# Ends of a sparse GATv2 layer: three per half block where there were five

## The chip, the cores and the metric

The kernel runs on one core of a Trainium2 chip. The metric is the device time of one execution in microseconds, as the median of ten runs: 3402.1 us before the change, with 3391.11 us the lowest and 3414.27 us the highest.

## What is computed

Two graph layers over 3327 nodes with 128 features, on one weighted adjacency matrix (`adj`, about 2% of its entries are not zero, the diagonal among them). The first is a GATv2 layer with four heads, the second a normalized graph convolution. Cut to what matters:

```python
h = maximum(layernorm(x), 0)
for each head:                      # w1, w2, a, Wlin of the head
    E = leaky_relu((h @ w1)[:, None, :] + (h @ w2)[None, :, :], 0.01)
    s = exp(tanh((E @ a) / 8) * 8) * adj
    s = s / sum(s, -1)
    out = leaky_relu(s @ h @ Wlin.T, 0.01)
x = x + concat(outs) @ w
# second layer
h = maximum(layernorm(x), 0)
x = x + relu(A_norm @ (h @ W.T + b))     # A_norm of adj + identity
```

## The kernel before

The rows are cut into 26 blocks of 128, and each block into two half blocks of 64 rows. For each row the kernel makes a list of its neighbours (`prep`, spread over the block before), and then works only on edges.

Each half block has five **parts**. Parts 0 to 3 hold 16 listed edges of each row each; part 4 holds the extra edges of rows with more. For parts 0 to 3, eight indirect DMAs on GpSimd (POOL, L595) gather 128 rows of a table in HBM, some 364 KB each, into one of four buffers `g`; part 4 has one buffer `ge`, two gathers and one plain DMA. A gathered row holds the features, the products with w2, a linear part of the score and the adjacency weights.

A half block is worked in nine **groups** `m`: parts 0 to 3 have two each (m = 0 to 7), part 4 has m = 8. For a group, `stage_z` turns the gathered rows (16 TensorE transposes, L622) into two PSUM tiles `z`, and VectorE takes the maximum with the row's own part into `r` (L638; ScalarE and VectorE share this for m = 8, L635 and L633). `stage_r` multiplies `r` by the vector `a` (L657). It does so for two groups at once, and a half group late: the scores of m = 0 and 1 are issued in the middle of group 2. One score matmul has two columns of weights, takes 512 columns of `r` and writes two PSUM rows for one head; four heads lie in four bands of 32 rows of one bank `s`, which is kept for the whole kernel. Row 0 is of the first group, row 1 of the second:

```python
for at, r in ((0, k.held), (1, rs)) if at else ((0, rs),):
    for h in range(H):
        nc.tensor.matmul(k.s[32 * h:32 * h + 2, :n], sel[:, h, 31 - at:33 - at], r[h // 2][:, h % 2, :n],
                         start=(at == 0), stop=(at == 1 or m == 8))
```

After each part comes its **end**, `finish`, a generator. It copies the bank to SBUF (`ssb`, ScalarE, L666), transposes it (L675, four matmuls, three for part 4), adds the linear parts (`sc`, VectorE, L678 and L681), takes tanh and exp (ScalarE, L686 and L688), multiplies with the adjacency weights (`wq` and `wt`, L670 and L697; `am` and `wo`, L713 and L715, for part 4), and multiplies with the gathered features into the PSUM tile `ag` (TensorE, L706, or L724 for part 4). Then `allow` gives the gather buffer back, and the next gather into it can be issued.

The order of instructions is written by hand. `slot()` is called six times for each group; it takes one step of every open generator (`tails`, `ends`), then of `prep`, then starts fetches for which a buffer is free. A `yield` in an end is one slot of distance: the products L706 stand twelve slots behind the start of their end, five of them behind `wt`. A fetch is made in the fixed order of blocks, halves and parts.

Other work in the same queues: `prep` transposes a block of `adj` (L365) and copies it out (`at`, ScalarE, L367, then a DMA from ScalarE's queue, L370); `known_step` uses `at` on TensorE (L379); `weights` writes a block's weights into the table (a DMA on SP's queue, L605); `close` ends a half block (L735 to L797). After the last block the second layer's strips come in through the same four buffers `g` (L898, from SP's and ScalarE's queues) and are multiplied (L988).

Of the kernel before, what the change touches and what calls it, by code (L numbers as in the profile page):

```python
# [9 lines left out]
F32 = mybir.dt.float32  # L10
AF = mybir.ActivationFunctionType
OP = mybir.AluOpType
# [3 lines left out]
P = 128  # L16
SLOPE = 0.01
CAP = 8.0
EPS = 1e-5
BANK = 512  # L20
# [42 lines left out]
OVT = 3  # L63
FOUND = 2
FEAT = 64
BODY = 648
# [3 lines left out]
WIDE = 712  # L70
WORK = 133
# [160 lines left out]
def _sparse_layers(tc, nc, x, adj, w1, w2, a, wlin, w, gw, gb, gb_sb, gwT, x_sb, dinv, flag, ident, out):  # L232
# [13 lines left out]
    NP, D = x.shape  # L246
    H = w1.shape[0]
# [4 lines left out]
    NG = 9  # L252
    WT = 8
    NW = NT // WT
    LATE = 1

    with ExitStack() as l0:
        res = l0.enter_context(tc.tile_pool(name="res", bufs=1))
# [9 lines left out]
        w1_sb = res.tile([P, H, D], F32, name="w1_sb")  # L268
        wlinT = res.tile([P, H, D], F32, name="wlinT")
        w_sb = res.tile([P, H, D], F32, name="w_sb")  # L270
        sel = res.tile([P, H, 33], F32, name="sel")
        p_all = res.tile([P, NB, 2 * H], F32, name="p_all")
        code = res.tile([P, NP], mybir.dt.uint16, name="code")
        epos = res.tile([P, 2 * FOUND], F32, name="epos")
# [3 lines left out]
        qmask = res.tile([P, 8], F32, name="qmask")  # L278
# [365 lines left out]

        def stage_r(k, hb, m, rs):
            n = 4 * P if m < 8 else FOUND * P + HALF
            at = m % 2
# [4 lines left out]
            if at == 0 and m < 8:  # L652
                k.held = rs
                return
            for at, r in ((0, k.held), (1, rs)) if at else ((0, rs),):
                for h in range(H):
                    nc.tensor.matmul(k.s[32 * h:32 * h + 2, :n], sel[:, h, 31 - at:33 - at], r[h // 2][:, h % 2, :n],  # L657
                                     start=(at == 0), stop=(at == 1 or m == 8))


        def finish(k, hb, w):
            g, s = k.g.pop((hb, w)), k.s
            f0 = k.f0[hb]
            nt, nk, nm = (WT, 4, 2) if w < NW else (OVT, OVT, 1)
            ssb = ph.tile([P, BANK], F32, name="ssb", bufs=1)
            nc.scalar.copy(ssb[:, :nk * P], s[:, :nk * P])  # L666
            if w < NW:
                wq = pb.tile([P, WT, 8], F32, name="wq")
                diag = bass.AP(g.tensor, g.offset + BODY * hb, [list(g.ap[0]), [WIDE + 8, 8], [1, 8]])
                nc.vector.tensor_tensor(wq, diag, qmask[:, None, :].to_broadcast([P, WT, 8]), OP.mult)  # L670
            yield
            yield
            pt = ps_tr.tile([P, 4, P], F32, name="tr")
            for q in range(nk):
                nc.tensor.transpose(pt[:, q, :], ssb[:, q * P:(q + 1) * P], ident)  # L675
            yield
            sc = pb.tile([P, WT, H], F32, name="sc")
            nc.vector.tensor_tensor(sc[:, :nt].rearrange("p (m k) h -> p m k h", m=nm),  # L678
                                    pt.rearrange("p k (h m) -> p m k h", m=32)[:, :nm, :nk],
                                    g[:, :, f0 + D:f0 + D + H].rearrange("p (m k) h -> p m k h", m=nm), OP.add)  # L680
            nc.vector.tensor_add(sc[:, :nt], sc[:, :nt], k.pex[:, 8 * hb:8 * hb + 8] if w < NW else  # L681
                                 k.ex[:, OVT * hb:OVT * hb + OVT, 42:42 + H])
            yield
            yield
            th = pb.tile([P, WT, H], F32, name="th")
            nc.scalar.activation(th[:, :nt], sc[:, :nt], AF.Tanh, scale=1.0 / CAP)  # L686
            pe = pb.tile([P, WT, H], F32, name="pe")
            nc.scalar.activation(pe[:, :nt], th[:, :nt], AF.Exp, scale=CAP)  # L688
            yield
            yield  # L690

            if w == 0:
                k.ag = ps_a.tile([P, 2, 256], F32, name="ag")
            ag = k.ag
            if w < NW:
                wt = pv.tile([P, WT, H, 8], F32, name="wt", bufs=2)
                nc.vector.tensor_tensor(wt, pe[:, :, :, None].to_broadcast([P, WT, H, 8]),  # L697
                                        wq[:, :, None, :].to_broadcast([P, WT, H, 8]), OP.mult)
                yield
                yield  # L700
                yield
                yield
                yield
                for t in range(WT):
                    u, cg = t // 4, t % 4
                    nc.tensor.matmul(ag[32 * cg:32 * cg + 32, u, :WORK], wt[:, t].rearrange("p h q -> p (h q)"),  # L706
                                     g[:, t, f0:f0 + WORK], start=(w == 0 and t < 4), stop=False, skip_group_check=True)
                allow("g")
                return
            am = pb.tile([P, OVT, HALF], F32, name="am", bufs=1)  # L710
            wo = pv.tile([P, OVT, 8, H, 8], F32, name="wo")
            for t in range(OVT):
                nc.vector.scalar_tensor_tensor(am[:, t, :], code[:, :HALF], k.ex[:, OVT * hb + t, 41:42], g[:, t, BODY * hb:BODY * hb + HALF],  # L713
                                               op0=OP.is_equal, op1=OP.mult)
                nc.vector.tensor_tensor(wo[:, t], pe[:, t, None, :, None].to_broadcast([P, 8, H, 8]),  # L715
                                        am[:, t].rearrange("p (g q) -> p g q", q=8)[:, :, None, :].to_broadcast([P, 8, H, 8]), OP.mult)
# [10 lines left out]
            tails.append(close(k, hb))  # L727


        def close(k, hb):  # L730
# [71 lines left out]
        blks = []  # L802
        for b in range(NB):
            k = Blk()
            k.f0 = FEAT, 0
            k.g, k.b, k.ready, k.turned, k.closed = {}, b, False, False, False
            blks.append(k)
        NCODE = 20
        NLIST = 42
        NPREP = 72  # L810
# [7 lines left out]
        ends, tails = [], []  # L818
# [183 lines left out]
        with tc.tile_pool(name="pre", bufs=1) as pre, ExitStack() as images:  # L1002
# [11 lines left out]
            room = [images.enter_context(tc.tile_pool(name=f"image{i}", bufs=1)).tile(  # L1014
                        [P, min(4, NB - 4 * i), BODY], F32, name=f"img{i}") for i in range(-(-NB // 4))]
# [176 lines left out]
        with tc.manual_schedule():  # L1192
            fetch()
            while queue:
                issue()
            rs = {}
            n = len(groups)
            def scores(i):
                if 0 <= i < n:
                    b, hb, m = groups[i]  # L1200
                    stage_r(blks[b], hb, m, rs.pop(i))
                    if m % 2 or m == NG - 1:
                        ends.append(finish(blks[b], hb, m // 2))
# [160 lines left out]
```

## Time and profile before

| | |
|---|---|
| median of ten runs | 3402.1 us (3391.11 to 3414.27) |
| the profiled execution | 3406.0 us, span 3404.3 us |
| mean granted TensorE clock | 0.88 |
| PE, PEld, DVE, ACT, POOL busy | 78%, 55%, 62%, 20%, 50% |
| DMA, mean | 243 GB/s, 826.94 MB moved |
| gathers on POOL (L595, `g`) | 1664 x 954 ns |
| maximum into `r` (L638) | 832 x 1218 ns |
| copy of the bank (L666) | 260 x 564 ns |
| transposes of the ends (L675) | 988, 172.2 us busy |
| products (L706) | 3328, 235.8 us busy |

PE is TensorE's matmuls, PEld its weight loads, DVE VectorE, ACT ScalarE. A group's line gives the line of the kernel, engine, operation, what is written from what, the number of instructions, then the busy time and the mean of one in ns, then the idle time of the engine just before them with what ended it. In a timeline a row gives start and length in us and, in brackets, the idle time before. An fp32 score matmul counts twice in the number of instructions.

### The profile page before, as it was taken

What the parts mean: (1) busy time and instruction counts of PE and PEld (TensorE: products, weight loads), DVE (VectorE), ACT (ScalarE), POOL (GpSimd) and SP (SyncE); (2) the same over time, 40 slices, a digit from 0 to 9 for tenths busy, and PEclk for the clock granted to TensorE, in tenths of its full rate; (3) what the DMA queues carried; (4) which work ended last, traced back from release to release, by engine and by line L of the source; (5) the groups of instructions that cost most, each with busy time, mean ns of one, the idle gap of its engine ahead of it and who ended that gap; (6) DMA issues with size and microseconds to landing.
All of it is one profiled execution on the core that took longest, in us unless ns stands there. A gap on an engine that the chain in (4) does not pass through costs nothing.

```text
span 3404.3 us, 52385 instructions
## 1 busy us (share of the span) xinstructions
PE 2641.9 (78%) x19410; PEld 1857.6 (55%) x19410; DVE 2099.0 (62%) x6426; ACT 683.0 (20%) x1703; POOL 1710.3 (50%) x1822
## 2 busy tenths in 40 slices
PE   6687777787777877787787777777787777777887
PEld 4465555555555555565555555555555555555553
DVE  6676666657656666666665665665665665665442
ACT  3122122212212212221121121221221221221110
POOL 3555555555555555545545545545545445445520
PEclk8788889988989889889888888988988888898999
DMA  9977778678777767867867867777777777777886
GB/s 325 319 253 260 227 249 268 216 238 275 234 227 262 253 214 251 263 202 251 268 201 244 264 209 237 255 226 227 251 231 224 250 234 222 231 223 222 268 257 185
DMA packets 417844, 826.94 MB, mean 243 GB/s; under 512 B 38435, under 2 KB 288815, under 8 KB 414255
## 3 DMA queue, kind: packets, MB, share of 16 engines
q0 software_dynamic: 141440, 619.41, 55.6%
q1 hardware_dynamic: 165343, 147.87, 14.1%
q10 hardware_dynamic: 110800, 56.25, 5.6%
q8 instruction: 156, 2.56, 0.3%
q14 instruction: 105, 0.86, 0.1%
HBM read 754.47 MB, written 113.22 MB: 255 GB/s over the span
## 4 chain that ended last, share of the span: by engine, by line
PE 51%; DVE 17%; issue 11%; another core or an unknown queue 11%; DMA 5%; POOL 3%; ACT 1%; ACTq 0%; SPq 0%; DVEq 0%; POOLq 0%
PE z L622 18%; PE s L657 10%; DVE r L638 9%; PE ag L706 5%; POOL g L595 3%; PE z L627 3%; PE tr L675 2%; DVE cand L422 2%; PE tr L379 2%; PE ag L724 2%; DMA g<-table,idx 2%; DMA g<-AT_d 1%; PE z L988 1%; PE tr L523 1%
## 5 line engine op out<-in xcount | busy, mean ns | idle before, releaser
L595 POOL DMA_INDIRECT g<-table,idx x1664 | 1588.1, 954 | 1361.4 <-PE ag L706 789.4
L638 DVE TENSOR_TENSOR r<-z,x1n 128x1024 f32<-128x1024 f32 x832 | 1013.0, 1218 | 871.0 <-remote 390.9
L622 PE MATMUL z<-ident,g 128*128 128x128 f32 x6656 | 1062.6, 305 | 182.4 <-issue 121.6
L622 PEld LDWEIGHTS z<-ident,g 128*128 128x128 f32 x6656 | 870.0, 159 | 366.1 <-issue 246.8
L657 PE MATMUL s<-r,sel 128*2 128x512 f32 (+1 forms) x3744 | 545.7, 609 | 134.9 <-DVE r L638 96.0
L666 ACT COPY ssb<-s 128x512 f32<-128x512 f32 x260 | 146.6, 564 | 843.7 <-PE s L657 303.2
L706 PE MATMUL ag<-g,wt 128*32 128x133 f32 x3328 | 235.8, 309 | 96.1 <-issue 95.3
L657 PEld LDWEIGHTS s<-r,sel 128*2 128x2 f32 x3744 | 82.6, 84 | 400.2 <-issue 254.3
L706 PEld LDWEIGHTS ag<-g,wt 128*32 128x32 f32 x3328 | 137.5, 119 | 219.9 <-issue 210.5
L675 PE MATMUL tr<-ident,ssb 128*128 128x128 f32 x988 | 172.2, 300 | 94.4 <-issue 76.3
L422 DVE MAX8 cand<-codes 128x8 f32<-128x52 uint16 x1664 | 217.3, 204 | 0.0
L675 PEld LDWEIGHTS tr<-ident,ssb 128*128 128x128 f32 x988 | 129.2, 155 | 120.4 <-issue 101.1
L595 POOL DMA_INDIRECT ge<-table,idxo x104 | 99.1, 952 | 182.6 <-PE ag L724 91.7
L379 PE MATMUL tr<-at,x_sb 128*128 128x128 f32 x488 | 99.2, 361 | 115.1 <-ACT at L367 109.6
L367 ACT COPY at<-tr 128x512 f32<-128x512 f32 (+1 forms) x175 | 97.2, 555 | 421.3 <-remote 219.5
L379 PEld LDWEIGHTS tr<-at,x_sb 128*128 128x128 f32 x488 | 83.4, 255 | 142.0 <-ACT at L367 130.9
L686 ACT ACTIVATE th<-sc 128x32 f32<-128x32 f32 x260 | 58.4, 225 | 499.0 <-DVE sc L681 234.7
L633 DVE TENSOR_TENSOR r<-z,x1n 128x128 f32<-128x128 f32 x104 | 30.1, 290 | 193.0 <-PE z L627 135.0
L365 PE MATMUL tr<-ident,adjb 128*128 128x128 f32 x676 | 124.3, 311 | 31.1 <-DMA adjb<-in_adj_dram 16.4
L627 PE MATMUL z<-oi,x1b 128*128 128x256 f32 x416 | 134.9, 408 | 4.0 <-issue 4.0
L453 DVE MAX8 lists<-cand 128x8 f32<-128x272 f32 (+1 forms) x338 | 133.3, 394 | 2.2
L622 PE MATMUL z<-ident,ge 128*128 128x128 f32 x416 | 87.7, 289 | 44.6 <-issue 32.8
(199 smaller groups left out, 2614.1 us busy)
## 6 DMA issues: line engine op xcount, KB each, us to landing
adjb<-in_adj_dram SPq DMA_DIRECT2D x26, 1664.0 KB
table<-AT_d SPq DMA_DIRECT2D x26, 1664.0 KB
AT_d<-at ACTq DMA_DIRECT2D x150, 256.0 KB
g<-table,idx POOLq DMA_INDIRECT x1664
table<-img SPq DMA_DIRECT2D x12, 1296.0 KB
adjb<-AT_d SPq DMA_DIRECT2D x72, 128.0 KB
g<-AT_d SPq DMA_DIRECT2D x25, 256.0 KB
g<-AT_d ACTq DMA_DIRECT2D x25, 256.0 KB
```

What stands on the lines that cost most here:

```text
L365: nc.tensor.transpose(pt[:, q, :], adjb[:, (j0 + q) * P:(j0 + q + 1) * P], ident)
L379: nc.tensor.matmul(pq[:, :P], x_sb[:, j0 + q, :], at[:, q, :], start=(q == 0), stop=(q == js[-1]))
L422: nc.vector.max(cand[:, c, 8:].rearrange("p (r s) -> p r s", s=32)[:, :, sgm % 32], codes.rearrange("p a b -> p (a b)")[:, sgm % 32 * SEG: ...
L453: nc.vector.max(top, of)
L595: return nc.gpsimd.indirect_dma_start(out=g[:, t, lo:hi], out_offset=None, in_=tab, in_offset=bass.IndirectOffsetOnAxis(ap=at[:, t:t + 1], ...
L622: nc.tensor.matmul(z[:, i, q * P:(q + 1) * P], g[:, m % 2 * 4 + q, c0:c0 + D], ident, is_transpose=True, start=(q == 0 or m < 8), stop=(m ...
L627: nc.tensor.matmul(z[:, i, :n], k.x1b[:, h * D:(h + 1) * D], k.oi[:, hb * n:(hb + 1) * n], start=False, stop=True, skip_group_check=True)
L638: nc.vector.tensor_tensor(r.rearrange("p h (i s) -> p h i s", s=16), z.rearrange("p h (i s) -> p h i s", s=16), k.x1n[:, 2 * hp:2 * hp + 2 ...
L657: nc.tensor.matmul(k.s[32 * h:32 * h + 2, :n], sel[:, h, 31 - at:33 - at], r[h // 2][:, h % 2, :n], start=(at == 0), stop=(at == 1 or m == 8))
L666: nc.scalar.copy(ssb[:, :nk * P], s[:, :nk * P])
L675: nc.tensor.transpose(pt[:, q, :], ssb[:, q * P:(q + 1) * P], ident)
L706: nc.tensor.matmul(ag[32 * cg:32 * cg + 32, u, :WORK], wt[:, t].rearrange("p h q -> p (h q)"), g[:, t, f0:f0 + WORK], start=(w == 0 and t ...
```

## The change

Parts 0 and 1 share one end, part 2 keeps its own, and parts 3 and 4 share one. The bank `s` now takes four rows of each band: a score matmul has four columns of weights, of which one is not zero, so that it writes its own row and adds nothing to the other three; the first of a bank has `start` set. `ROWS` says for the group at which scores are issued in which row they begin and whether the bank is complete, `ENDS` after which group an end starts and for which parts. An end handles up to 16 tiles at once in `sc` and `pe`; tanh is taken in place. The products are in `weigh` and `gather_extras`, which one end runs side by side, and stand `GAP` = 3 slots behind `wt`. The bank is always copied with 512 columns and turned with four transposes.

```diff
-        sel = res.tile([P, H, 33], F32, name="sel")
+        sel = res.tile([P, H, 35], F32, name="sel")
...
-            for at, r in ((0, k.held), (1, rs)) if at else ((0, rs),):
+            at, last = ROWS[m]
+            for row, r in ((at, k.held), (at + 1, rs)) if m < 8 else ((at, rs),):
                 for h in range(H):
-                    nc.tensor.matmul(k.s[32 * h:32 * h + 2, :n], sel[:, h, 31 - at:33 - at], r[h // 2][:, h % 2, :n],
-                                     start=(at == 0), stop=(at == 1 or m == 8))
+                    nc.tensor.matmul(k.s[32 * h:32 * h + 4, :n], sel[:, h, 31 - row:35 - row], r[h // 2][:, h % 2, :n],
+                                     start=(row == 0), stop=(last and (m == 8 or row > at)), skip_group_check=True)
...
+        def weigh(k, hb, w, at, pe, wq):
+            g, f0 = k.g.pop((hb, w)), k.f0[hb]
+            wt = pv.tile([P, WT, H, 8], F32, name="wt", bufs=2)
+            nc.vector.tensor_tensor(wt, pe[:, at:at + WT, :, None].to_broadcast([P, WT, H, 8]),
+                                    wq[:, :, None, :].to_broadcast([P, WT, H, 8]), OP.mult)
+            for _ in range(GAP):
+                yield
+            for t in range(WT):
+                u, cg = t // 4, t % 4
+                nc.tensor.matmul(k.ag[32 * cg:32 * cg + 32, u, :WORK], wt[:, t].rearrange("p h q -> p (h q)"),
+                                 g[:, t, f0:f0 + WORK], start=(w == 0 and t < 4), stop=False, skip_group_check=True)
+            allow("g")
...
+        def finish(k, hb, ws):
+            s, f0 = k.s, k.f0[hb]
+            ssb = ph.tile([P, BANK], F32, name="ssb", bufs=1)
+            nc.scalar.copy(ssb, s)
+            lists_of = [w for w in ws if w < NW]
+            for w in lists_of:
...
+                nc.vector.tensor_tensor(k.wq[w], diag, qmask[:, None, :].to_broadcast([P, WT, 8]), OP.mult)
+            yield
+            yield
+            pt = ps_tr.tile([P, 4, P], F32, name="tr")
+            for q in range(4):
+                nc.tensor.transpose(pt[:, q, :], ssb[:, q * P:(q + 1) * P], ident)
+            yield
...
+            for i, w in enumerate(ws):
...
+                nc.vector.tensor_tensor(of, by_row[:, 2 * i:2 * i + nm, :nk],
+                                        k.g[hb, w][:, :, f0 + D:f0 + D + H].rearrange("p (m k) h -> p m k h", m=nm), OP.add)
...
+            nc.scalar.activation(sc[:, :tiles], sc[:, :tiles], AF.Tanh, scale=1.0 / CAP)
+            pe = pb.tile(room, F32, name="pe")
+            nc.scalar.activation(pe[:, :tiles], sc[:, :tiles], AF.Exp, scale=CAP)
+            yield
+            yield
...
+            parts = [gather_extras(k, hb, WT * i, pe) if w == NW else weigh(k, hb, w, WT * i, pe, k.wq.pop(w)) for i, w in enumerate(ws)]
+            while parts:
+                parts = [f for f in parts if next(f, "end") != "end"]
+                yield
...
+        GAP = 3
+        WIDTH = 2 * WT
+        ENDS = {3: (0, 1), 5: (2,), 8: (3, 4)}
+        ROWS = {1: (0, False), 3: (2, True), 5: (0, True), 7: (0, False), 8: (2, True)}
...
-                    if m % 2 or m == NG - 1:
-                        ends.append(finish(blks[b], hb, m // 2))
+                    if m in ENDS:
+                        ends.append(finish(blks[b], hb, ENDS[m]))
```

More of the change, by code (lines that the diff above doesn't have):

```diff
@@ L646, in stage_r @@
             n = 4 * P if m < 8 else FOUND * P + HALF
-            at = m % 2
             if state["scores"] is None:
@@ L651, in stage_r @@
             k.s = state["scores"]
-            if at == 0 and m < 8:
+            if m % 2 == 0 and m < 8:
                 k.held = rs
                 return
-            for at, r in ((0, k.held), (1, rs)) if at else ((0, rs),):
+            at, last = ROWS[m]
+            for row, r in ((at, k.held), (at + 1, rs)) if m < 8 else ((at, rs),):
                 for h in range(H):
-                    nc.tensor.matmul(k.s[32 * h:32 * h + 2, :n], sel[:, h, 31 - at:33 - at], r[h // 2][:, h % 2, :n],
-                                     start=(at == 0), stop=(at == 1 or m == 8))
@@ L661, in finish @@
[L661 to L698, printed above, removed]
-                yield
[L700 to L709, printed above, removed]
@@ L710, in finish, with gather_extras @@
+        def gather_extras(k, hb, at, pe):
+            g, f0, ag = k.g.pop((hb, NW)), k.f0[hb], k.ag
             am = pb.tile([P, OVT, HALF], F32, name="am", bufs=1)
@@ L714, in finish @@
                                                op0=OP.is_equal, op1=OP.mult)
-                nc.vector.tensor_tensor(wo[:, t], pe[:, t, None, :, None].to_broadcast([P, 8, H, 8]),
+                nc.vector.tensor_tensor(wo[:, t], pe[:, at + t, None, :, None].to_broadcast([P, 8, H, 8]),
                                         am[:, t].rearrange("p (g q) -> p g q", q=8)[:, :, None, :].to_broadcast([P, 8, H, 8]), OP.mult)
@@ L727, in finish @@
             tails.append(close(k, hb))
+        def finish(k, hb, ws):
[4 more added lines that the diff above has]
+            for w in lists_of:
+                g = k.g[hb, w]
+                k.wq[w] = pb.tile([P, WT, 8], F32, name="wq")
+                diag = bass.AP(g.tensor, g.offset + BODY * hb, [list(g.ap[0]), [WIDE + 8, 8], [1, 8]])
+                nc.vector.tensor_tensor(k.wq[w], diag, qmask[:, None, :].to_broadcast([P, WT, 8]), OP.mult)
[5 more added lines that the diff above has]
+            yield
+            room = [P, WIDTH, H]
+            sc = pb.tile(room, F32, name="sc", bufs=1)
+            by_row = pt.rearrange("p k (h m) -> p m k h", m=32)
+            tiles = 0
+            for i, w in enumerate(ws):
+                nt, nk, nm = (WT, 4, 2) if w < NW else (OVT, OVT, 1)
+                of = sc[:, WT * i:WT * i + nt].rearrange("p (m k) h -> p m k h", m=nm)
+                nc.vector.tensor_tensor(of, by_row[:, 2 * i:2 * i + nm, :nk],
+                                        k.g[hb, w][:, :, f0 + D:f0 + D + H].rearrange("p (m k) h -> p m k h", m=nm), OP.add)
+                tiles += nt
+            if len(lists_of) == 2:
+                of = sc[:, :tiles].rearrange("p (i t) h -> p i t h", i=2)
+                nc.vector.tensor_tensor(of, of, k.pex[:, None, 8 * hb:8 * hb + 8].to_broadcast([P, 2, WT, H]), OP.add)
+            else:
+                nc.vector.tensor_add(sc[:, :WT], sc[:, :WT], k.pex[:, 8 * hb:8 * hb + 8])
+            if NW in ws:
+                nc.vector.tensor_add(sc[:, WT:tiles], sc[:, WT:tiles], k.ex[:, OVT * hb:OVT * hb + OVT, 42:42 + H])
+            yield
[5 more added lines that the diff above has]
+            yield
+            if 0 in ws:
+                k.ag = ps_a.tile([P, 2, 256], F32, name="ag")
+            parts = [gather_extras(k, hb, WT * i, pe) if w == NW else weigh(k, hb, w, WT * i, pe, k.wq.pop(w)) for i, w in enumerate(ws)]
+            while parts:
+                parts = [f for f in parts if next(f, "end") != "end"]
+                yield
@@ L805, in _sparse_layers @@
             k.f0 = FEAT, 0
-            k.g, k.b, k.ready, k.turned, k.closed = {}, b, False, False, False
+            k.g, k.wq, k.b, k.ready, k.turned, k.closed = {}, {}, b, False, False, False
             blks.append(k)
+        GAP = 3
+        WIDTH = 2 * WT
+        ENDS = {3: (0, 1), 5: (2,), 8: (3, 4)}
+        ROWS = {1: (0, False), 3: (2, True), 5: (0, True), 7: (0, False), 8: (2, True)}
         NCODE = 20
```

## The prediction

> **What bounds the kernel now.** I read the busy shares, then the chain that ended last, then the groups of the lines that change, then the timelines of PE, ACT and POOL over one half block.
>
> ```profile
> PE 2641.9 (78%) x19410; PEld 1857.6 (55%) x19410; DVE 2099.0 (62%) x6426; ACT 683.0 (20%) x1703; POOL 1710.3 (50%) x1822
> PE 51%; DVE 17%; issue 11%; another core or an unknown queue 11%; DMA 5%; POOL 3%; ACT 1%; ACTq 0%; SPq 0%; DVEq 0%; POOLq 0%
> L675 PE MATMUL tr<-ident,ssb 128*128 128x128 f32 x988 | 172.2, 300 | 94.4 <-issue 76.3 <-ACT ssb L666 11.6 <-DMA g<-table,idx 6.2
> L666 ACT COPY ssb<-s 128x512 f32<-128x512 f32 x260 | 146.6, 564 | 843.7 <-PE s L657 303.2
> ```
>
> PE is the busiest engine and carries half of the chain. It stands idle for 743 us in all (its gaps in the timeline), and 94.4 us of that lie ahead of L675, the transposes of the ends. The 11% under an unknown queue is a stall that the profile doesn't explain; it comes back below.
>
> Where do the 94.4 us sit? I sorted the gaps ahead of the first L675 transpose by which of the five ends of a half block it belongs to: part 0 has 36.6 us (26 of 52 ends, all in the second half of a block), parts 1, 2 and 3 together 0.2, the extra edges 57.6 (49 of 52 ends). The next two fences, PE's timeline and ACT's, show one of the latter.
>
> ```profile
> 1558.70 0.72 PE L657 MATMUL s<-r,sel 128*2 128x320 f32 x8
> 1559.35 1.09 PE L622 MATMUL z<-ident,g 128*128 128x128 f32 x8
> 1562.36 0.55 PE L675 MATMUL tr<-ident,ssb 128*128 128x128 f32 x3 [1.92 <-issue]
> ```
>
> ```profile
> 1558.19 0.23 ACT L686 ACTIVATE th<-sc 128x32 f32<-128x32 f32 x1 [0.38 <-issue]
> 1558.45 0.23 ACT L688 ACTIVATE pe<-th 128x32 f32<-128x32 f32 x1
> 1561.83 0.48 ACT L666 COPY ssb<-s 128x384 f32<-128x384 f32 x1 [3.15 <-PE z L622]
> ```
>
> PE does eight z transposes after the extra edges' scores and then waits 1.92 us for the copy of the bank. On ACT the copy stands behind part 3's tanh and exp, which wait for part 3's sums. Ends 1 to 3 have 16 more matmuls (L706, the products of the part before) between scores and transposes, and don't wait.
>
> DVE is not what PE follows: when PE reaches the first z of a group, the `r` that freed its bank has mostly been done for several us. POOL waits for PE instead:
>
> ```profile
> POOL g L595 <- PE ag L706: 789.4, 164, 8.8
> DVE r L638 <- remote: 390.9, 115, 9.6
> ```
>
> So gathers come early: the rows of a group have landed 15 to 25 us before PE needs them in nearly all halves.
>
> **The change, part by part**, on the profiled execution (3406.0 us, span 3404.3). Two ends fewer in each of 52 half blocks.
>
> *PE work.* Transposes fall from 988 (four ends of four, one of three) to 52 x 12 = 624, 364 fewer. By the row, 172.2 / 988 = 174 ns each: 63 us. The floor is the spacing inside a run of four, (0.60 - 0.27) / 3 = 0.11 us: 40 us. Part 0's end of the second halves (26 x 4 = 104 transposes) goes from a stretch where ACT's `at` copies set the pace ("PE tr L379 <- ACT at L367" is 109.6 us); there I give nothing. That leaves 260 x 0.174 = 45 us. Score matmuls stay 3744 with the same streamed columns; four weight columns for two go through an 84 ns weight load that overlaps: nothing, at most a few ns each.
>
> *Waits ahead of the transposes.* Part 0's 36.6 us have the same `at` cause, so I count none; PE would wait a little later. For the extra edges' 57.6 us, part 3's tanh and exp no longer stand ahead of the copy in ACT's order; m == 8's own relu does, and the scores wait for that anyway. The copy can then start 0.05 us after the scores, as it does for part 1's end, and takes 0.585 us (512 columns for 384) against eight z transposes, 0.87 us: covered. 49 of these waits could go; half of them lie at the start of the second half, where `at` sets the pace, so I take 57.6 / 2 = 29 us. Ends: 0 and 94.
>
> *Lost cover.* The joint end of parts 0 and 1 and the end of part 2 no longer have L706 between scores and transposes. In the trace the copy was done 0.5 to 0.7 us (10th percentile) before parts 1's and 2's transposes came; an L706 run takes 0.5 to 0.65 us. So mostly just covered: 104 x 0.05 = 5 us. If the whole mean run counts (235.8 / 208 = 1.13 us), 0.45 x 104 = 47 us; the near rows say the former.
>
> *DVE.* wq, wt, am and wo keep their number. Sums go from ten instructions (4 x (185 + 192) + 166 + 171 = 1.85 us) to nine, 1.7 us by the same rows with some 220 ns for the wide add: 8 us in all, off PE's path, counted 0. Bunched, they delay an `r` by at most one 415 ns wt more; the lead above covers that. Without the lead it would cost 0.4 x 52 = 21 us.
>
> *A new wait.* GAP = 3 puts the products three slots behind wt in place of five, so their first matmul now waits for wt, and z, scores and the next release of a buffer queue behind it. In the trace of before, PE comes to the new places 3.8 us or more after the `r` that precedes wt, what follows it and wt are done: 0. If DVE were last, wt (0.4 to 0.8 us) and the small work ahead of it (up to 0.9) would be waited for three times a half: up to 200 us.
>
> *ACT.* Two copies and four small activations fewer, 585 + 478 and some 840 ns per half, 99 us at 20% busy: 0 beyond the waits above.
>
> *Gathers.* Part 0's buffer is now released with part 1's, 1.7 groups later in order, some 7 us in the halves that I read; then 16 gathers stand on POOL in a row at 1.25 us (0.95 busy + 0.30 between), and a gather lands 4.2 us after issue (packets of queue 0, 80 for each gather; 6 to 12 us where table writes run). Moving each part's margin by its shift leaves at least 4.1 us (the second group of part 0, median 12.6) and at least 7.5 for all others: 0. SP's table write is queued after part 1's gathers as before, one third of a group earlier.
>
> *Tail.* In the last half two strips are freed together, so ACT issues twelve strip DMAs at once (6.5 + 7.0 us in place of two blocks), ahead of the last `r` L635. That wait was 5.97 us already. I take +3 (from -4 to +7).
>
> Sum: -45 - 29 + 5 + 3 = -66, so 3340 profiled. The median stands 3.9 us below the profiled run: **3336 us**. The ends: the chain gives L675 2.4% (82 us), of which 364 / 988 is 30 us, a floor for the gain if no wait goes; all busy time and all waits give 63 + 94 = 157.
>
> [...]
>
> **Rivals.**
> *The gain is absorbed.* Time that PE saves comes back as a wait for `at`, for `r`, or in the unexplained stall. For it: DVE and the stall hold 28% of the chain. Against it: PE's lead over DVE is short nowhere. Then only small change is left, -10 to +10: about 3402.
>
> *Gathers run late.* If 16 in a row bring the worst landing seen (11.8 us) to every burst, eight gathers in flight give 11.8 / 8 = 1.47 us cadence; part 0's last row then comes 7.6 + 7 x 0.22 = 9.1 us late, which exceeds the margin in about a third of halves, 0.8 us on average: 41 us, so 3377. It would need landings of 16 us to turn the sign.
>
> *Slower: more of the unexplained stall.* At 1575.5 PE's eight z are modelled to end at 1576.5, but DVE is released at 1578.3 ("remote"); the times between PE's semaphore events there come in multiples of 1.43 us. 11% of 3404 us is 7.2 us a half, about five such steps. They often follow dense runs: L724 with L675 and z, or L706. The change makes a denser one, two L706 runs back to back. One step more in each half costs 52 x 1.43 = 74 us and eats the gain; from there on it is slower, and with one and a half, 112 - 66 = +46: 3448. Against it: 364 matmuls and as many weight loads fewer.
>
> **How the numbers follow.** My forecast 0.60; absorbed 0.13; late gathers 0.07; slower 0.20. A measurement tells about 0.3% (10 us) from no change. The forecast's own range is 3402 - 157 to 3402 - 30 with lost cover, 3250 to 3390; cut at its thin lower end and stretched over the absorbed case and the beginning of the slower one it is 3275 to 3420. Faster: 0.60 + 0.07 + 0.02 of the absorbed = 0.69; same 0.11; slower 0.20.
>
> **What would show it.** Right: the transposes' group at x624 with under 50 us of idle time before it; PE busy some 60 us less; no DMA wait ahead of z; ACT busy near 585 us; halves of about 61 us where they were 62. Wrong: idle time ahead of the products or of z that grows by over 60 us; z released by a gather; "remote" ahead of `r` above 450 us; a mean granted clock under 0.87.

## The result, and the profile after

The changed kernel takes 4128.8 us (median, 4113.64 to 4140.91) beside 3406.0 us for the kernel before in the same comparison: 1.212 times as long, interval 1.210 to 1.214. The profiled execution takes 4102.4 us with a span of 4100.7 us; the mean granted TensorE clock is 0.80, it was 0.88.

How far the two kernels differ depends on where they run. The later comparisons ran on several chips, and they fall into two kinds. On the **first kind** (chips 0, 7, 8 and 14) the kernel before takes 3277 to 3421 us, as here. On the **second kind** (chips 5, 11 and 12) it takes 2501 to 2503 us, and there the changed kernel is only 1.2% slower. The recorded result is of the first kind by its times, and so is everything below that isn't said to be of the second. Only chip 0 came in two comparisons (both times of the first kind), so whether it is the chip or its condition at the time isn't shown.

The lines that answer to those of before, from the page of the changed kernel (busy shares, chain, the groups of the transposes and of the copy):

```profile
PE 2614.1 (64%) x19046; PEld 1830.5 (45%) x19046; DVE 2085.7 (51%) x6374; ACT 592.9 (14%) x1391; POOL 1730.1 (42%) x1822
PE 23%; another core or an unknown queue 9%; issue 8%; DVE 8%; DMA 2%; ACT 1%; ACTq 0%; DVEq 0%; SPq 0%
L709 PE MATMUL tr<-ident,ssb 128*128 128x128 f32 x624 | 122.6, 330 | 323.5 <-ACT ssb L698 225.7
L698 ACT COPY ssb<-s 128x512 f32<-128x512 f32 x156 | 91.5, 586 | 752.9 <-remote 406.1
```

and from its waits:

```profile
POOL g L595 <- PE ag L670: 1638.1, 152, 17.4
DVE r L638 <- remote: 920.2, 157, 15.9
```

No engine became the bound: all busy shares fell. The transposes are 624 as foretold, but the idle time ahead of them grew from 94.4 to 323.5 us, and "remote" ahead of `r` from 390.9 to 920.2. The chain can be followed back to 2003.6 us only, so it tells of the second half of the span alone, and its shares add up to 51%. One stretch of the timeline (PE, DVE and the first and last POOL row of a run of gathers) shows them:

```profile
1110.85 0.95 POOL L595 DMA_INDIRECT g<-table,idx  x1 [16.03 <-PE ag L670]
...
1114.30 1.09 PE L622 MATMUL z<-ident,g 128*128 128x128 f32 x8
...
1116.34 1.04 PE L622 MATMUL z<-ident,g 128*128 128x128 f32 x8
...
1118.11 1.23 DVE L638 TENSOR_TENSOR r<-z,x1n 128x1024 f32<-128x1024 f32 x1 [3.63 <-PE z L622]
...
1119.39 1.97 PE L622 MATMUL z<-ident,g 128*128 128x128 f32 x8 [2.02 <-issue]
...
1129.62 0.94 POOL L595 DMA_INDIRECT g<-table,idx  x1 [0.30 <-issue]
...
1132.19 1.23 DVE L638 TENSOR_TENSOR r<-z,x1n 128x1024 f32<-128x1024 f32 x1 [9.05 <-remote]
1133.47 0.69 PE L622 MATMUL z<-ident,ge 128*128 128x128 f32 x2 [12.11 <-issue]
```

Parts 0 and 1 come free together, so POOL issues 16 gathers without a pause, from 1110.85 to 1130.56. Eight transposes stand at 1114.30 with 1.09 us, yet the `r` that waits for them starts at 1118.11. The next eight stand at 1116.34, and their `r` starts at 1132.19, 14.8 us after their modelled end. The `r` of the eight after those starts at 1134.08, when the run is over. The rows that these transposes read had landed long before: leaving out the first and last few half blocks, the first transpose of a gathered row stands at least 15 us after the row's landing.

The clock is not the reason. The windows of another run of 16 (behind the window's length stand the busy us and the instructions of PE, PEld, DVE, ACT and POOL, then the granted clock, the DMA share and GB/s) show TensorE at full clock while it comes to a stop; the clock falls afterwards:

```profile
1186.00:1191.00 5.00, 4.60 (x40) 2.80 (x38) 3.90 (x14) 0.49 (x1) 3.78 (x5) 1.00 0.65 192
1191.00:1196.00 5.00, 1.50 (x12) 1.29 (x12) 0.35 (x1) 0.50 (x2) 3.78 (x5) 1.00 0.86 277
1196.00:1201.00 5.00, 0.00 (x0) 0.00 (x0) 0.00 (x0) 0.00 (x0) 3.78 (x5) 0.69 0.86 280
1201.00:1206.00 5.00, 0.00 (x0) 0.00 (x0) 0.00 (x0) 0.39 (x1) 3.29 (x4) 0.50 0.89 281
```

To measure this over a whole trace I set each matmul that posts a semaphore beside the event of that semaphore. About half of the events come within 0.02 us of the matmul's modelled end. Of those that come over 0.3 us after it, some nine in ten lie in unbroken runs of gathers (1.25 us apart), and in them this **lag** grows from the third or fourth gather on until about 2 us after the last. This is the median, over runs of one length, of the largest lag in a run:

| kernel (kind of chip) | gathers in the run (runs) | largest lag, us |
|---|---|---|
| before, recorded (first) | 2 (55), 8 (199) | 0.1, 5.0 |
| after, recorded (first) | 8 (73), 10 (28), 16 (49) | 5.4, 7.8, 14.9 |
| e5_paced_before (first) | 2 (232), 4 (90), 6 (73), 8 (50) | 0.0, 2.0, 3.9, 5.2 |
| e1_third_chip (first) | 8 (97), 16 (51) | 4.6, 14.2 |
| e1_joint_release (second) | 8 (6), 13 (18), 21 (11) | 0.0, 0.0, 0.0 |

So on the first kind of chip the TensorE's completions fall behind by about 1.1 us for each gather of a run after the third, and a run of two shows next to none. On the second kind the lag stays under 0.3 us.

### The profile page after: what moved, and what is told of

Same layout as the page of the kernel before. It is cut to its first block, busy times and chain, and to the rows that moved or that the text cites. A ratio compares the mean times of both kernels' runs of the same rounds, so it can differ in the third digit from the quotient of the medians.

```text
span 4100.7 us, 51264 instructions
## 1 busy us (share of the span) xinstructions
PE 2614.1 (64%) x19046; PEld 1830.5 (45%) x19046; DVE 2085.7 (51%) x6374; ACT 592.9 (14%) x1391; POOL 1730.1 (42%) x1822
## 3 DMA queue, kind: packets, MB, share of 16 engines
q0 software_dynamic: 141440, 619.41, 46.1%
## 4 chain that ended last, share of the span: by engine, by line
PE 23%; another core or an unknown queue 9%; issue 8%; DVE 8%; DMA 2%; ACT 1%; ACTq 0%; DVEq 0%; SPq 0%
PE z L622 8%; PE s L657 4%; DVE r L638 4%; PE ag L670 2%; PE tr L379 1%; DMA g<-AT_d 1%; PE z L627 1%; PE tr L709 1%; DVE cand L422 1%; PE z L1006 1%; PE tr L365 1%; PE tr L942 1%; PE tr L771 1%; DVE codes L410 1%
## 5 line engine op out<-in xcount | busy, mean ns | idle before, releaser
L638 DVE TENSOR_TENSOR r<-z,x1n 128x1024 f32<-128x1024 f32 x832 | 1013.8, 1219 | 1364.5 <-remote 920.2
L622 PE MATMUL z<-ident,g 128*128 128x128 f32 x6656 | 1112.8, 313 | 668.3 <-issue 387.6
L657 PE MATMUL s<-r,sel 128*4 128x512 f32 (+1 forms) x3744 | 490.6, 608 | 16.7 <-issue 11.0
L709 PE MATMUL tr<-ident,ssb 128*128 128x128 f32 x624 | 122.6, 330 | 323.5 <-ACT ssb L698 225.7
L709 PEld LDWEIGHTS tr<-ident,ssb 128*128 128x128 f32 x624 | 83.1, 165 | 347.9 <-ACT ssb L698 239.9
L622 PEld LDWEIGHTS z<-ident,ge 128*128 128x128 f32 x416 | 55.6, 165 | 355.6 <-issue 194.6
L698 ACT COPY ssb<-s 128x512 f32<-128x512 f32 x156 | 91.5, 586 | 752.9 <-remote 406.1
L657 PEld LDWEIGHTS s<-r,sel 128*4 128x4 f32 x3744 | 82.2, 87 | 257.6 <-issue 239.4
L670 PE MATMUL ag<-g,wt 128*32 128x133 f32 x3328 | 154.3, 321 | 7.8 <-DVE wt L664 5.6
L635 ACT ACTIVATE r<-z 128x512 f32<-128x512 f32 x104 | 62.0, 597 | 593.5 <-DVE r L633 450.0
L365 PE MATMUL tr<-ident,adjb 128*128 128x128 f32 x676 | 129.7, 323 | 25.9 <-DMA adjb<-in_adj_dram 15.9
L670 PEld LDWEIGHTS ag<-g,wt 128*32 128x32 f32 x3328 | 97.3, 123 | 62.0 <-issue 25.4
```

Of the source, the lines that this page charges most:

```text
L365: nc.tensor.transpose(pt[:, q, :], adjb[:, (j0 + q) * P:(j0 + q + 1) * P], ident)
L622: nc.tensor.matmul(z[:, i, q * P:(q + 1) * P], g[:, m % 2 * 4 + q, c0:c0 + D], ident, is_transpose=True, start=(q == 0 or m < 8), stop=(m ...
L638: nc.vector.tensor_tensor(r.rearrange("p h (i s) -> p h i s", s=16), z.rearrange("p h (i s) -> p h i s", s=16), k.x1n[:, 2 * hp:2 * hp + 2 ...
L657: nc.tensor.matmul(k.s[32 * h:32 * h + 4, :n], sel[:, h, 31 - row:35 - row], r[h // 2][:, h % 2, :n], start=(row == 0), stop=(last and (m ...
L670: nc.tensor.matmul(k.ag[32 * cg:32 * cg + 32, u, :WORK], wt[:, t].rearrange("p h q -> p (h q)"), g[:, t, f0:f0 + WORK], start=(w == 0 and ...
```

## The experiments

Theory A is this: the joint release makes runs of 16, and runs hold TensorE back. Rival B is that the joint ends themselves cost the time, rival C that rows come late. A2 is A with what the first comparison taught, that how far TensorE falls behind depends on the chip. The times before and the ratios are those of each comparison.

**The joint release alone, in the kernel before.** Part 0's products wait until those of part 1; the five ends stay.

```diff
-                yield
-                yield
-                yield
-                yield
-                yield
+                for _ in range(5 + (12 if w == 0 else 0)):
+                    yield
                 for t in range(WT):
```

> The kernel before with its five ends per half block, in which only the eight products of part 0 are put off by 12 steps, so that they stand beside those of part 1 and both buffers come free together, as in the changed kernel. Theory A (gather runs: in an unbroken run of row gathers the TensorE's completions fall behind from the third or fourth gather on, by about 1 us per gather, until the run has landed; a joint release makes runs of 16 in place of 8): 4000 to 4250 us, runs of 16 gathers in the trace, TensorE behind by up to 15 us at their end. Rival B (the joint ends themselves: fewer and larger ends crowd the copies, the bank and VectorE): within 50 us of 3406, since the ends are untouched. Rival C (rows come too late): slower only if the time from landing to the first transpose goes below zero for some part.

> The kernel of e1_joint_release again (five ends as in the kernel before, the products of part 0 put off by 12 steps so that two buffers come free together), for a chip on which TensorE falls behind in gather runs. Theory A2: there, runs of 16 stop TensorE for about 16 us in place of twice 4 to 6, so 5 to 10 us more per half block and 1.08 to 1.16 of the kernel before. Rival B: the ends are untouched, 1.00 to 1.04. On a chip on which TensorE does not fall behind: 1.037 as before.

> The kernel of e1_joint_release once more (five ends as in the kernel before, only part 0's products 12 steps later, beside those of part 1). On a chip on which TensorE falls behind, theory A2: runs of 16 and 1.08 to 1.20 of the kernel before; rival B: 1.00 to 1.04. On a chip on which it does not: 1.037.

The first two ran on the second kind: 2595.4 beside 2502.0 us (1.037, interval 1.035 to 1.039) and 2592.3 beside 2501.1 (1.038, 1.035 to 1.040). The absolute times that the first expectation names are therefore missed; it was written before I knew of two kinds. The loss there fits rival C. The chain by engine and by line, and the wait of the transposes for gathered rows, are

```profile
PE 34%; DMA 19%; POOL 19%; DVE 18%; issue 8%; SPq 0%; ACT 0%; ACTq 0%; DVEq 0%; POOLq 0%
POOL g L595 19%; DMA g<-table,idx 14%; PE z L622 11%; DVE r L638 9%; PE s L657 9%; DVE cand L422 4%; PE ag L703 2%; PE z L627 2%; DVE codes L410 2%; DMA g<-AT_d 1%; PE z L985 1%; PE tr L675 1%; PE z L1103 1%; DMA adjb<-in_adj_dram 1%; PE tr L754 1%
PE z L622 <- DMA g<-table,idx: 70.5, 95, 2.6
```

with 33% on gathers and what issues them. In about half of the half blocks a row lands 1 us or less ahead of its first transpose, and the transposes wait 70.5 us for rows. In e3_apart_01, which has no joint release, rows land 6 us or more ahead in every half block but the first, and that wait is 8.0 us. The third ran on the first kind: 3686.2 beside 3276.9 us, **1.126** (1.121 to 1.131). It has 51 runs of 16, and a lag of 14.2 us at their end. Its rows land 8 us or more ahead in every half block but the first, so rival C is out on this kind. The release alone, with every end untouched, is enough for more than half of the loss.

**The joint release taken out of the changed kernel.** Parts 1, 2 and 3 make their products later, so that buffers come free one by one; the three ends stay. The diff is that of the two runs of e2; e8_staggered_5 has `GAP` = 5 besides, and 0 for part 3. e10_joint_5 has `GAP` = 5 and nothing else.

```diff
-            for _ in range(GAP):
+            for _ in range(GAP + LATER[w]):
...
+        LATER = {0: 0, 1: 11, 2: 9, 3: 2}
```

> The changed kernel with three ends per half block, in which only the products of parts 1, 2 and 3 come 11, 9 and 2 steps later, so that the four buffers come free 10 to 11 steps apart. Theory A: no run longer than 8 gathers, 3300 to 3420 us. Rival B: the ends are those of the changed kernel, so 4050 to 4150 us. Rival C: later releases leave less time for the rows, so it is slower than the changed kernel, above 4150 us.

> The kernel of e2_staggered again (three ends as in the changed kernel, the products of parts 1, 2 and 3 put off by 11, 9 and 2 steps so that the buffers come free one by one), for a chip on which TensorE falls behind in gather runs. Theory A2: there, no run is longer than 8 to 10 and the time is within 8% of the kernel before (at most 1.08 of it, where the changed kernel took 1.21): three runs or four per half block at 4 to 5 us each. Rival B (the joint ends cost the time there): 1.15 or more. On a chip on which TensorE does not fall behind: 1.01 as before.

> The changed kernel with its three ends, the products five steps after their weights as in the kernel before (the change has three), and those of parts 1 and 2 put off by 11 and 9 steps more, so that the four buffers come free one by one. Theory A2: on a chip on which TensorE falls behind in gather runs, no run over 10 and at most 1.08 of the kernel before, where the changed kernel took 1.21; rival B (the joint ends cost the time): 1.15 or more. On a chip on which it does not fall behind: 1.00 to 1.02.

> The changed kernel with the products five steps after their weights as in the kernel before, and nothing else: the three ends and the joint release of parts 0 and 1 stay. Against e8_staggered_5 (1.039 of the kernel before on chip 0) it differs in the joint release alone. Theory A2: on a chip on which TensorE falls behind, runs of 16 gathers and 1.15 to 1.25 of the kernel before. If the three steps in place of five were what cost the time (f1_five_ends had them, with single releases, and took 1.098): 1.02 to 1.08. On a chip on which it does not fall behind: 1.01 to 1.02.

Both runs of e2 came to the second kind, where the length of a run holds nothing back: 1.011 (1.009 to 1.013) and 1.012 (1.010 to 1.013). On the first kind, e8_staggered_5 takes 3542.2 beside 3420.8 us, **1.039** (1.032 to 1.046), and e10_joint_5 takes 3749.5 beside 3276.9 us, **1.143** (1.138 to 1.149), just under what A2 named. The two differ only in where the products of parts 1 and 2 stand, and so in the joint release: 1.143 / 1.039 = 1.10. e8 has one run longer than ten, e10 has 52. And e10 differs from the changed kernel in the steps alone: 1.212 / 1.143 = 1.06. Both factors are loose, since the three ratios come from three comparisons, and the times before differ by 4% between those of e8 and e10, both on chip 0. By the times of the kernels alone they are 3749.5 / 3542.2 = 1.06 and 4128.8 / 3749.5 = 1.10.

**One joint end undone, and all.**

```diff
-        ENDS = {3: (0, 1), 5: (2,), 8: (3, 4)}
+        ENDS = {1: (0,), 3: (1,), 5: (2,), 8: (3, 4)}             # e3_apart_01
+        ENDS = {1: (0,), 3: (1,), 5: (2,), 7: (3,), 8: (4,)}      # f1_five_ends
```

> The changed kernel with parts 0 and 1 given ends of their own again (four ends per half block); part 3 and the extra edges still share one. Theory A: runs of 8 again, 3340 to 3410 us, a little under the kernel before for the 52 ends of extra edges that are gone. Rival B: the shared end of part 3 and the extra edges has the longest waits of its transposes (206 us in the changed kernel), so much of the loss stays: 3700 us or more.

> The changed kernel with a table that gives each of the four parts and the extra edges an end of its own again (five per half block), all else as changed: score rows of 4, products three steps after their weights, the new functions. Theory A2: the buffers come free one by one as in the kernel before, runs of 8 gathers; so it takes the time of the kernel before within 1.5% on a chip of either kind (3360 to 3460 us where that takes about 3400, 2480 to 2540 us where it takes about 2500). Rival B2 (something else in the rewrite, the wider score rows or the earlier products, costs the time): above 3700 us on the first kind, 2530 us or more on the second.

e3_apart_01 ran on the second kind: 2529.3 beside 2502.0 us, 1.011 (1.009 to 1.012). It says nothing on the first. f1_five_ends ran on the first: 3613.9 beside 3281.8 us, **1.098** (1.091 to 1.105), and here theory A missed: single releases, 203 runs of 8, a lag of 4.9 us as in the kernel before, and still 10% slower. So something besides the length of runs counts.

**Products three steps after `wt` in place of five, in the kernel before.** Two of the five `yield` lines go.

> The kernel before with the products three steps after their weights in place of five, and nothing else: five ends, single releases. f1_five_ends, which had that besides the wider rows and the new functions, took 1.098 of the kernel before where TensorE falls behind in gather runs. If the earlier products are what cost it there, because the run then begins at another place of the order and its end meets a VectorE that has nothing left: 1.05 to 1.11. If it is the wider rows or the new functions: 0.99 to 1.02. Where TensorE does not fall behind: 0.99 to 1.02 either way.

3577.6 beside 3277.8 us: **1.093** (1.086 to 1.100). These two steps account for f1_five_ends: what is left for the wider score rows and new functions is 0.5%, less than the intervals can tell. The groups of the transposes and the products, first of before_again, then of g1_before_3, show how:

```profile
L675 PE MATMUL tr<-ident,ssb 128*128 128x128 f32 x988 | 172.0, 299 | 112.0 <-issue 90.7 <-ACT ssb L666 14.4 <-DMA g<-table,idx 6.9
L706 PE MATMUL ag<-g,wt 128*32 128x133 f32 x3328 | 236.8, 309 | 94.3 <-issue 92.9
```

```profile
L675 PE MATMUL tr<-ident,ssb 128*128 128x128 f32 x988 | 173.1, 300 | 248.0 <-ACT ssb L666 235.5 <-issue 12.0
L704 PE MATMUL ag<-g,wt 128*32 128x133 f32 x3328 | 189.5, 362 | 8.8 <-DVE wt L697 4.3
```

The products don't wait for `wt` (4.3 us in all). But they stand earlier, so they no longer lie between an end's scores and its transposes, and the run that they release begins earlier too. The wait for the copy grows from 14.4 to 235.5 us. The lag at the end of runs of 8 is 5.0 us, as before, so the runs are no worse; that their late part now meets scores, copy and transposes is my reading, and no run tests it. The two groups together are idle for 50 us more, out of a loss of 300.

**The two kernels again.**

> The changed kernel once more, unchanged, because the kernel before took 2502 us in the last comparison, on chip 5, where 3402 to 3406 us had been measured before, and TensorE's completions were never over 0.3 us behind there. Theory A2 (the loss of 720 us comes from gather runs, and how far TensorE falls behind in them depends on the chip or its condition): where the kernel before takes about 2500 us, the changed one takes 2570 to 2630 us (+3 to +5%, about what the joint release alone cost), with TensorE not behind in runs of 16; where the kernel before takes about 3400 us, 4100 to 4150 us with TensorE behind by up to 16 us. Rival B (the joint ends cost the time on any chip): +15% or more in both.

> The kernel before itself, for its trace on this chip. Theory A2: if it takes about 2500 us, TensorE's completions stay within 0.3 us of their modelled ends in every run of gathers; if it takes 3200 us or more, they fall behind by 4 to 6 us at the end of runs of 8.

after_again, on the second kind, takes 2533.6 beside 2502.9 us, 1.012 (1.010 to 1.015). Its page:

```profile
PE 2230.2 (88%) x19046; PEld 1547.2 (61%) x19046; DVE 2049.9 (81%) x6374; ACT 590.2 (23%) x1391; POOL 1745.3 (69%) x1822
PE 29%; DVE 28%; DMA 20%; POOL 13%; issue 7%; SPq 1%; ACT 0%; DVEq 0%; ACTq 0%; POOLq 0%
L709 PE MATMUL tr<-ident,ssb 128*128 128x128 f32 x624 | 95.2, 276 | 14.1 <-ACT ssb L698 14.1
```

It is the same program, 51264 instructions, in 2540 us in place of 4101. The transposes wait 14.1 us here in place of 323.5, with runs of up to 68 gathers. The loss is less than A2 foretold (3 to 5%) and far from B's 15%. before_again, on the first kind, takes 3414.0 us, with a lag of 5.2 us at the end of runs of 8.

**Gathers spread in pairs.** Each two gathers read their row numbers from a copy that VectorE makes every third step, so they can't run ahead of VectorE (in e5_paced_before POOL waits 391.1 us for these copies).

```diff
+                    ic = pv.tile([P, 2], mybir.dt.int32, name="ic", bufs=4)
+                    nc.vector.tensor_copy(ic, at[:, t:t + 2])
+                    one(t, ic[:, :1])
+                    return one(t + 1, ic[:, 1:])
...
+            pairs = 9 if state["slot"] < 24 else state["slot"] % 3 == 0
```

> The changed kernel with its joint ends and joint release, in which each two gathers read their row numbers from a small copy that VectorE makes at every third step, so that the gathers go out in pairs spread over the half block (884 more VectorE copies of 2 numbers). Theory A: no run over 2 to 4 gathers, TensorE no longer behind, 2950 to 3300 us, under both kernels. Rival B: about 4100 us, the ends being the same. A third view (the mean rate of about 200 GB/s is already what TensorE suffers from, not the run): 3900 us or more.

> The kernel before, in which each two gathers read their row numbers from a small copy that VectorE makes at every third step, so that they go out in pairs spread over the half block (884 more VectorE copies of 2 numbers). Theory A2: where the kernel before takes about 3400 us and TensorE falls behind in runs of 8, 2600 to 3100 us, with TensorE no longer behind; where it takes about 2500 us there is nothing to gain from pairs, and the later rows and the copies cost 2 to 6%, 2550 to 2650 us. If on the first kind the mean rate and not the run is what holds TensorE, 3400 us or more there.

> The kernel of e5_paced_before again (gathers in pairs behind small VectorE copies). Where TensorE falls behind in gather runs: 0.93 to 0.98 of the kernel before once more. Where it does not: 1.03 to 1.06, since the pairs then only make the rows later, as e4_paced_after was 1.051.

> The kernel of e5_paced_before (gathers in pairs behind small VectorE copies), in which a part's buffer is handed to the next gathers five steps after its products, so that a copy is not made before the buffer is free and the pairs do not pile up into runs of 6 and 8. Theory A2: where TensorE falls behind in runs, nearly all runs are of 2 to 4 and the time is 0.85 to 0.95 of the kernel before, below e5_paced_before's 0.955; where it does not, 1.04 to 1.08. If the mean rate is what holds TensorE: 0.95 to 1.02 on the first kind.

e4_paced_after, on the second kind, takes 1.051 (1.050 to 1.053), where the changed kernel took 1.012: with nothing to gain, the pairs only cost time. Later rows are a small part of it: z's transposes wait 37.9 us for them (18.6 in parts 0 to 3, 19.3 in part 4) beside 28.3 us in after_again (26.2 and 2.1), 10 us of the 97 between the two medians. On the first kind e5_paced_before takes 3147.9 beside 3281.8 us, **0.955** (0.948 to 0.962), and again 3144.6 beside 3279.2, **0.960** (0.956 to 0.965): faster than both kernels there. It was expected under 3100 us, because I took all runs to become pairs; 50 runs of 8 and 73 of 6 are left. e9_paced_later, meant to break those too, is a miss: 3374.6 beside 3277.8 us, 1.030 (1.023 to 1.038). It has 96 runs of 8, more than e5, so it did not do what it was for.

**Fewer bytes, as many gathers.**

```diff
                     lo, hi = (8 * t, hi) if hb == 0 else (0, BODY + 8 * t + 8)
+                    if hb == 0:
+                        hi -= 2 * D
+                    else:
+                        lo += 2 * D
```

> The changed kernel, whose gathers leave out the last two heads' 256 numbers of each row (first block half) or the first 256 (second), some 38% of their bytes; ScalarE writes a constant there instead, 8x256 numbers per part, so the result is another. The number and the order of the gathers stay. Theory A2 with the bytes as the cause: where the kernel before takes about 3400 us, this one takes 2800 to 3300 us, TensorE not behind; where it takes about 2500 us, 2350 to 2550 us, since there the DMA engines are busy 90% of the time. If the issue of the gathers on GpSimd is what slows TensorE, and not their bytes: about 4100 us on the first, about as the changed kernel on the second.

> The kernel before with gathers that leave out 256 of each row's numbers, some 38% of their bytes (ScalarE writes a constant in their place, so the result is another); the number and the order of gathers stay. Where TensorE falls behind in runs: if the bytes in flight are the cause, 0.80 to 0.92 of the kernel before and TensorE less than 2 us behind at the end of runs of 8; if the issue or the completion signals of the gathers are, 0.98 to 1.04 and 4 to 6 us behind. Where it does not: 0.97 to 1.02.

e6_fewer_bytes, on the second kind, takes 1.009 (1.006 to 1.012) and tells little. e7_fewer_bytes, on the first, takes 3298.8 beside 3277.8 us: 1.007 (1.003 to 1.011). Queue 0 of before_again and then of e7 (packets, MB, share of 16 engines):

```profile
q0 software_dynamic: 141440, 619.41, 55.9%
```

```profile
q0 software_dynamic: 114816, 401.31, 43.6%
```

A third of the bytes is gone (227 KB for a gather in place of 350), and the lag at the end of runs of 8 is 4.2 us in place of 5.2. So it doesn't go by the bytes. It fell as much as the packets did (114816 / 141440 = 0.81, 4.2 / 5.2 = 0.81); whether they set it isn't tested. The edit isn't pure: the gathers now wait for ScalarE's constant too, and 393.8 us of POOL's waits are put down to ScalarE's copy of the bank, where before_again has none.

## Why the prediction was wrong

*The step that failed: gathers counted as 0.* I asked of a later release only whether rows come in time, and moved each margin by its shift. That part held on the first kind, where rows landed 15 us or more ahead, in halves that had grown by 13.4 us (4100.7 - 3404.3, over 52). On the second kind, where halves are shorter, a row of after_again lands 1 us or less ahead in about 20 of 52. What I didn't ask is what 16 gathers in a row do to TensorE. The joint release that I put at 0 costs a factor of 1.126 alone, in the kernel before (e1_third_chip). Summed over a half block by the table, the largest lags were 199 x 5.0 / 52 = 19 us before and (73 x 5.4 + 28 x 7.8 + 49 x 14.9) / 52 = 26 us after. That is some 7 of the 13.4 us; the rest I put down to where the runs fall, and no run measures that apart.

*The slower rival had the right place and the wrong cause and size.* In the stretch that I quoted, the "unexplained stall" was this lag. I tied it to dense TensorE work and priced it at one or one and a half steps of 1.43 us in each half; with the 66 us that I counted as gain, it was (696 + 66) / 52 / 1.43 = ten steps. VectorE is released there at 1578.3, and the last gather of a run of 8 ends on POOL at 1576.7: the row was there, one engine further down, and I didn't set it beside the stall. Its chance of 0.20, and the range's upper end of 3420 us, rested on that price.

*Waits ahead of the transposes, -29, and lost cover, +5.* Here the first kind of chip shows 323.5 us where I expected under 50. g1_before_3 shows the sign of the error: with no end joined, two steps less lift the wait from 112.0 to 248.0 us. I measured the cover in modelled ends, which TensorE doesn't keep in a run. On the second kind, where it does, 14.1 us are left, and both terms fit. But this wait doesn't tell the loss. The transposes' groups of e8_staggered_5 (1.039) and then e10_joint_5 (1.143):

```profile
L709 PE MATMUL tr<-ident,ssb 128*128 128x128 f32 x624 | 121.0, 327 | 300.1 <-ACT ssb L698 180.9 <-issue 119.2
L709 PE MATMUL tr<-ident,ssb 128*128 128x128 f32 x624 | 109.5, 304 | 123.8 <-ACT ssb L698 108.8 <-issue 14.8
```

*TensorE's work, -45.* 364 transposes are gone, as counted. PE's busy time fell by 27.8 us only (2641.9 to 2614.1), at a mean clock of 0.80 in place of 0.88: the mean of z's transposes rose from 305 to 313 ns, that of the ends' from 300 to 330.

*The new wait on `wt`, 0, and ScalarE.* Right: 5.6 us ahead of L670 are put down to `wt`, and ACT is busy 592.9 us where I said 585. But what the two steps moved was the release behind the products, and that I didn't price: 1.06 to 1.10.

*The signs I named.* "Remote" above 450 us (920.2), a clock under 0.87 (0.80) and more idle time ahead of z (182.4 to 668.3 us) all came; z released by a gather did not (4.6 us).

*The merging of the ends.* The waits ahead of the transposes don't follow it: e10_joint_5 has merged ends and 123.8 us, g1_before_3 separate ones and 248.0. With merged ends and single releases e8_staggered_5 is at 1.039, and e2_staggered at 1.011 on the second kind, which is all that is left for it.

So the factor of 1.21 is 1.06 to 1.10 for the joint release, as much for the earlier products (the two together 1.17) and 1.04 for the rest of the change. What stays open: the last 1.04 (1.01 on the second kind), how much of the loss is the length of the runs and how much their place, and what in a gather holds TensorE back, or whether the recording of the trace does (last section).

## What to carry to other kernels

When a buffer is released earlier, later or together with another, look at what the transfers then do as a group: put the DMA queue's rows beside the waits that the profile can't name, before asking whether the data is in time. A wait between engines that "remote" or "issue" ends is a finding to settle before a change is priced, since a price for it is a guess. And take the time of both kernels on more than one chip if there is a choice: here the same pair differs by 21% or by 1%.

## What the runs showed of the hardware

The same program took 2540 us on one chip and 4101 us on another. On the first kind of chip TensorE's completions come late in runs of gathers (14.9 us at the end of 16). The one signal between other engines that I measured does not suffer: ScalarE's tanh starts 0.03 us (median of 25) after VectorE's sum inside the late parts of before_again's runs, and 0.03 us outside them too. Whether TensorE works slowly there or only tells of it late, these traces can't say.

The records differ as well. Of the semaphore events of the 1768 gathers, the trace of after_again holds 28151, 15.9 for each, and that of the recorded changed kernel 9664, 5.5 for each, with all 51264 instructions in both. This goes with the kind of chip in all 20 traces: 9650 to 14009 events on the first, 27998 to 28205 on the second. Whether the recording holds TensorE back no run here shows: every timed execution was recorded, with its span and clock, so none tells the time without. That the lag comes from the recording, and not from the gathers, is therefore a rival that stays untested.
